# A selective-scan and feed-forward kernel on one Trainium2 core: scans from zero, first columns by ScalarE, shifted products, new places

## The chip, the cores and the metric

The kernel runs on one core of one Trainium2 chip. A core has five engines that run side by side: TensorE (PE in the profile; its weight loads are PEld), VectorE (DVE), ScalarE (ACT), GpSimd (POOL) and SyncE (SP, which here issues the DMAs). Each works through its own list of instructions in order, and an instruction waits on semaphores for what it needs from other engines and from DMAs. The metric is the device time of the program in microseconds (us), the median of several runs.

## The reference, cut to what matters

The input is two sequences of 4096 tokens with 256 features. The kernel computes a normalised selective-scan layer (Mamba-like) with a residual, and then a normalised feed-forward layer with ternary weights and a residual.

```python
xz = jnp.einsum('bld,ed->ble', x, W_in)            # x is layer-normed; 2 x 512 channels
x_path, z = jnp.split(xz, 2, axis=-1)
x_path = jax.nn.silu(x_path)
ssm = jnp.einsum('ble,se->bls', x_path, W_x)       # B, C (16 states each), dt, lam
...
dA = jnp.exp(A[None, None] * dt[..., None])
Bx = Br[:, :, None, :] * x_path[..., None]
u = (1.0 - lam_e) * dt_e * dA * Bx_prev + lam_e * dt_e * Bx
u = u.at[:, 0].set(dt_e[:, 0] * Bx[:, 0])
def step(h, inp):
    dA_, u_, C_ = inp
    h = dA_ * h + u_
    return (h, jnp.sum(h * C_[:, None, :], axis=-1))
_, ys = jax.lax.scan(step, h0, (dA_t, u_t, C_t))   # 512 channels x 16 states, 4096 steps
y = (y + x_path * D) * jax.nn.silu(z)
x = x + layernorm(einsum('ble,de->bld', y, W_out))
...
h = gelu(layer_norm(x) @ ternary(w1).T + b1)
x = x + layernorm(layer_norm(h) @ ternary(w2).T + b2)
```

## The kernel before

**Tiling.** The 8192 tokens are 16 blocks of T = 512 (`NB`), eight for each sequence; blocks 0 and 8 start a sequence (`s.first`). The scan of a block has 512 channels x 16 states = 8192 rows of 512 steps. A *unit* is one tile of 128 such rows: 32 channels (`G`) x 4 states. Block k has 64 units, numbered by j (four groups of 128 channels), q (four rounds of four states) and c (four sets of 32 channels within j). The four units of one (j, q) are a *group*; they share the tile `g` of 128 x 4 x 512, of which there are three (`GBUFS`).

**What a group does.** `decay` (ScalarE) makes da = exp(A dt) of one unit in PSUM, from the tile `dtr` (four decay tiles, `DA_PSUM`). `inputs` (GpSimd, L1046) makes the scan's input in `g`, the product of the tile `b` (the state's B, broadcast over the channels) and `vr` (the weighted x of the channels), in two halves of two units each. `unit_scan` (VectorE) runs the recurrence of a unit over the 512 steps with a starting value `ini`, a column of a small tile, or 0.0 in blocks 0 and 8. For the first `SPLIT[q]` units of a group (2, 1, 2, 1) the scan writes over da in PSUM (L1059), and VectorE multiplies it with C into `g` (`product_v`, L1076) and copies the last column into `hl` (L1077). For the other units the scan writes over `g` (L1062), ScalarE copies the last columns to `hl` (`last`, L1066), and GpSimd multiplies with C in place (`product_g`, L1072, 1024 or 1536 elements per partition). `sum_states` (TensorE, L1088) adds the states of a group by four matmuls into `y`, and `gate` (L1098) multiplies with silu(z). The tiles `b` and `c` are T + 2 columns wide and used from column 2.

**From block to block.** The state after the last step (`hl`) goes into the next block. Because u holds a term of the previous token, the start value is `hl` plus an outer product: `over`, `over_x`, `spread` and `carry` (L1023) make the outer product in the tile `ini`, and `initial` (GpSimd, L1032) adds `hl`, first for j = 0 and later for the rest.

**Order.** The instruction lists are written out by hand (`manual_schedule`); nothing is reordered afterwards. The main loop walks the units in order, and each unit has three *places*. While the scans of block k run, the front part of block k + 1 (`plan_ahead`: norm, projections, softplus, angles, B and C, the weighted x) and the back part of block k - 1 (`plan_behind`: output projection and the feed-forward layer) are issued piece by piece at the places of the table `AT` (192 places are one block); the front of block 0 takes its places from `AT_FIRST`, and the preparation of the ternary weights from `W_AT`. What belongs to a group comes at the lags of the table `LAG`, counted from the group's first unit. Decays and inputs are issued two units ahead of their scan (`AHEAD_DA`, `AHEAD_U`). The loads of `dtr` and `vr` for j + 1 (`load_ch`) stand in the main loop at the first unit of j, and the load of x of the block after the next at unit 60 (`X_AT`). All these DMAs go through SP's queue.

Of the kernel before, what the change touches and what calls it, by code (L numbers as in the profile page):

```python
# [8 lines left out]
F32 = mybir.dt.float32  # L9
# [5 lines left out]
P = 128  # L15
# [30 lines left out]
AHEAD_DA, AHEAD_U = 2, 2  # L46
X_AT = 60
# [4 lines left out]
    "product_v": (4,),  # L52
    "last": (24, 15, 21, 18, 13, 13, 18, 14, 19, 21, 21, 14, 15, 13, 19, 11),
    "product_g": (28, 17, 30, 19, 22, 17, 20, 26, 24, 21, 25, 20, 24, 13, 24, 15),
    "gate": (35, 38, 31, 26),
    "start": (18, 26, 27, 26),
    "sum": (32, 30, 36, 25, 36, 35, 24, 30, 31, 29, 28, 23, 45, 31, 29, 22),
}

W_AT = (1, 46, 70, 73, 74, 78, 85, 92, 103, 103, 106, 114, 116, 124, 141, 144, 149, 149, 153, 160, 160, 163, 163, 170, 174, 176, 180, 187, 188)  # L60
LOAD_FIRST = 6
AT = {
    "a_stats": (5, 5),
    "a_power": (5,),
    "a_offset": (8,),
    "a_apply": (8, 8),
    "a_turn": (15, 15),
    "a_evict": (16, 17),
    "project": (17, 24, 31, 31, 62, 66, 66, 76),
    "keep": (21, 25, 31, 35, 68, 72, 74, 78),  # L70
    "silu_x": (36,),
    "bc_project": (55, 60),
    "bc_take": (73,),
    "dt_project": (82,),
    "bc_square": (88,),
    "bc_power": (95,),
    "dt_row": (84,),
    "dt_spread": (92,),
    "softplus": (92,),
    "bc_scale": (137,),  # L80
    "dt_turn": (109, 115, 117, 117),
    "dt_keep": (117, 118, 118, 120),
    "dt_sum": (121,),
    "angles": (129,),
    "diag_lam": (118,),
    "silu_z": (153,),
    "sines": (153,),
    "rotate_a": (154,),
    "rotate_b": (154,),
    "bc_turn": (158,),  # L90
    "bc_store": (164,),
    "dot_sum": (176,),
    "dot_shift": (194,),
    "dot_take": (194,),
    "weigh": (141, 159, 194, 196),
    "weigh_x": (150, 167, 197, 197),
    "over": (121,),
    "over_x": (132,),
    "spread": (179,),
    "carry": (185,),  # L100
    "diag_dot": (196,),
    "skip": (198, 199, 199, 200),
    "skip_x": (198, 199, 200, 200),
    "load_dt": (124,),
    "load_v": (150,),
    "load_b": (167, 172, 172, 174),
    "load_c": (172, 184, 186, 189),
    "x_load": (4,),
    "out_project": (41, 49),
    "out_square": (47, 49),  # L110
    "out_power": (49, 54),
    "residual": (53, 54),
    "h_stats": (58, 58),
    "h_power": (63,),
    "h_offset": (65,),
    "h_apply": (68, 69),
    "h_turn": (78, 82),
    "h_evict": (78, 82),
    "ffn_1": (85, 93, 97, 98, 103, 107, 117, 129),
    "ffn_keep": (88, 94, 97, 106, 114, 115, 121, 135),  # L120
    "gelu": (133, 135),
    "ffn_2": (137, 150, 162, 190),
    "ffn_sums": (145, 159, 173, 191),
    "ffn_out": (146, 159, 175, 195),
    "ffn_square": (177, 160, 195, 196),
    "ffn_power": (180, 196),
    "ffn_scale": (189, 196),
    "finish": (189, 196),
# [3 lines left out]
    "a_stats": (-90, -90),  # L132
    "a_power": (-90,),
    "a_offset": (-90,),
    "a_apply": (-90, -90),
    "a_turn": (-90, -90),
    "a_evict": (-90, -90),
    "project": (-78, -77, -75, -72, 0, 12, 0, 3),
    "keep": (-76, -74, -71, -69, 0, 16, 0, 9),
    "silu_x": (-58,),  # L140
    "bc_project": (-70, -70),
    "bc_take": (-67,),
    "dt_project": (-66,),
    "bc_square": (-61,),
    "bc_power": (-60,),
    "dt_row": (-65,),
    "dt_spread": (-64,),
    "softplus": (-63,),
    "bc_scale": (-59,),
    "dt_sum": (-53,),  # L150
    "dt_turn": (-55, -55, -55, -55),
    "dt_keep": (-55, -55, -55, -55),
    "angles": (-52,),
    "diag_lam": (-54,),
    "silu_z": (56,),
    "sines": (-50,),
    "rotate_a": (-47,),
    "rotate_b": (-46,),
    "bc_turn": (-45,),
    "bc_store": (-44,),  # L160
    "dot_sum": (-30,),
    "dot_shift": (0,),
    "dot_take": (0,),
    "weigh": (-51, 0, 0, 2),
    "weigh_x": (-49, 0, 4, 8),
    "diag_dot": (0,),
    "skip": (1, 9, 0, 0),
    "skip_x": (2, 12, 0, 0),
    "load_dt": (-62,),
    "load_v": (-42,),  # L170
    "load_b": (-43, -20, 0, 7),
    "load_c": (-41, -20, 5, 20),
    "bc_project_first": (-73, -70, -69, -68),
    "decay_rates": (-57,),
# [4 lines left out]
def mamba_ffn_kernel(  # L179
# [287 lines left out]
    def weights_2(wide):  # L467
# [13 lines left out]
        def gains(h):  # L481
            if h == 0:
                nc.vector.tensor_add(b2bc, t["pb"], b2bc)
                t["row"] = small.tile([P, NH + 1], F32, tag="row", name="row", bufs=1)
            for f in range(4 * h, 4 * h + 4):
                nc.scalar.activation(
                    w[:, f, :],
                    q[:, f, :],
                    AF.Copy,
                    scale=t["g"][:, f : f + 1],  # L490
                    accum_out=t["row"][:, f : f + 1],
                )
# [61 lines left out]
    class Norm:  # L554


        def __init__(self, src, scale, eps, name):
            self.src, self.scale, self.eps, self.name = src, scale, eps, name
            self.mv = small.tile([P, NC4, 2], F32, tag="mv", name=f"mv_{name}")
            self.st = small.tile([P, NC4, 6], F32, tag="st", name=f"st_{name}")  # L560

        def stats(self, cs):
            for c in cs:
                nc.vector.bn_stats(self.st[:, c, :], self.src[:, c, :])
                nc.vector.bn_aggr(self.mv[:, c, :], self.st[:, c, :])
# [21 lines left out]
        def turn(self, kk):  # L587
            if kk == 0:
                self.oT = p1.tile([P, 2, T], F32, tag="oT", name=f"oT_{self.name}")
                self.pt = {}  # L590
# [11 lines left out]
    class Centred(Norm):  # L602


        def __init__(self, src, sums, scale, eps, name):
            self.src, self.sums, self.scale, self.eps, self.name = src, sums, scale / DM, eps, name
            self.nm = small.tile([P, NC4], F32, tag="nm", name=f"nm_{name}")
# [19 lines left out]
    class Block:  # L627
        pass

    def new_block(k):  # L630
# [5 lines left out]
        s.pz, s.dt, s.dtT, s.dx, s.vs, s.ph, s.bcq, s.ch, s.g = {}, {}, {}, {}, {}, {}, {}, {}, {}  # L636
        s.p2, s.ff, s.pq, s.ps, s.ys = {}, {}, {}, {}, {}
# [14 lines left out]
    def keep(s, e):  # L652
        if e == 0:
            s.xp = p1.tile([P, NJ, T], F32, tag="xp", name=f"xp_{s.k}")
            s.zs = {}
# [18 lines left out]
    def bc_project(s, cs):  # L674

        if cs[0] == 0:
            s.pbc = ps_ff.tile([P, NC4, 2 * NS + 2], F32, tag="ff", name=f"pbc_{s.k}")
# [73 lines left out]
    def softplus(s):  # L751
        if s.k == 0:
            special(freqs, freqs, AF.Softplus)

            nc.vector.tensor_scalar_mul(freqs, freqs, 1.0 / DI)
        for j in range(NJ):
            dt = p1.tile([P, T], F32, tag="dt", name=f"dt_{s.k}_{j}", bufs=4)
            special(dt, s.pb, AF.Softplus, scale=wdt[:, j : j + 1], bias=bdt[:, j : j + 1])
            nc.sync.dma_start(s.dt_d[j * P : (j + 1) * P, :], dt)
            s.dt[j] = dt  # L760
# [19 lines left out]
    def dt_turn(s, c):  # L780

        s.pq[c] = mm_tile([P, DI], f"pdtT_{s.k}_{c}")
        for j in range(NJ):
            nc.tensor.transpose(
                s.pq[c][:, j * P : (j + 1) * P], s.dt[j][:, c * P : (c + 1) * P], ident
            )

    def dt_keep(s, c):
        if c == 0:
            s.msum = small.tile([P, NC4], F32, tag="msum", name=f"msum_{s.k}")  # L790
# [7 lines left out]
    def angles(s):  # L798
# [3 lines left out]
        tn = small.tile([P, NC4, H], F32, tag="turns", name=f"tn_{k}", bufs=1)  # L802
        s.ang = small.tile([P, NC4, H], F32, tag="ang", name=f"ang_{k}")
        acc = pa[:, 3, 0, 0:NC4]
        s.cum = small.tile([P, NC4], F32, tag="cum", name=f"cum_{k}")
        nc.vector.tensor_copy(s.cum, acc)
        nc.vector.tensor_mul(
            ang,
            acc[:, :, None].to_broadcast([P, NC4, H]),
            freqs[:, None, :].to_broadcast([P, NC4, H]),  # L810
        )
        nc.vector.tensor_scalar(turns, ang, INV_2PI, ROUND, ALU.mult, ALU.add)
        nc.vector.tensor_scalar_sub(tn, turns, ROUND)
        for part in (PI2_HI, PI2_MID, PI2_LO):
            nc.vector.scalar_tensor_tensor(ang, tn, -part, ang, ALU.mult, ALU.add)
        nc.vector.tensor_scalar(s.ang, ang, -3.1415925, 3.1415925, ALU.max, ALU.min)
# [46 lines left out]
    def bc_store(s):  # L863
# [3 lines left out]
        s.blast = small.tile([NS, NQ], F32, tag="blast", name=f"blast_{s.k}")  # L867
        nc.scalar.activation(s.blast, round_of, AF.Copy, scale=bct[0:NS, T - 1 : T])
# [56 lines left out]
    def weigh(s, j):  # L925
# [5 lines left out]
            rhs=s.dt[j][:, 1:],  # L931
# [6 lines left out]
    def weigh_x(s, j):  # L938
        v = p1.tile([P, T], F32, tag="v", name=f"v_{s.k}_{j}", bufs=2)
        nc.vector.tensor_mul(v, s.ps.pop(j), s.xp[:, j, :])  # L940
        nc.sync.dma_start(s.v_d[j * P : (j + 1) * P, :], v)
# [14 lines left out]
    def over_x(s, prev):  # L956
        c4 = small.tile([P, NJ], F32, tag="c4", name=f"c4_{s.k}")
        nc.vector.tensor_mul(c4, s.po4, prev.xlast)
        s.c4 = c4

    def spread(s, prev):

        s.pov = mm_tile([P, NJ * NG + NQ], f"pov_{s.k}")
        for c in range(NG):
            nc.tensor.matmul(
                s.pov[:, 0 : NJ * NG].rearrange("p (j c) -> p j c", c=NG)[:, :, c],
# [5 lines left out]
        nc.tensor.matmul(s.pov[:, NJ * NG :], lhsT=state, rhs=prev.blast, start=True, stop=True)  # L972
# [636 lines left out]
```

## Time and profile before

| | us |
|---|---|
| median of 3 runs (lowest, highest) | 2003.9 (1998.66, 2006.47) |
| span of the profiled execution | 2000.2 |
| VectorE busy, share of the span | 1765.9, 88% |
| TensorE busy | 1779.9, 89% |
| GpSimd busy | 1750.2, 88% |
| ScalarE busy | 1625.3, 81% |
| mean granted TensorE clock | 0.953 of full speed |
| DMA, share of the 16 engines (hardware queue) | 47.8%, 230.80 MB |

The profile is of one execution. Busy times are the union of an engine's instructions; the ends of matmuls are modelled, and instructions that only wait or issue DMAs are not counted. In its rows, `out<-in` names tiles, then come partitions x elements and the count, the busy time and the mean duration in ns, and behind the second bar the engine's idle time just before these instructions with what ended most of it. The lines with L230 are ScalarE's activations, all recorded by one helper.

### The profile page before, as it was taken

The numbers are of one execution on the slowest core, as the hardware profiler recorded it, in microseconds if no ns is written. First come the engines' busy times: TensorE is split into PE (matmuls) and PEld (weight loads), VectorE is DVE, ScalarE is ACT, GpSimd is POOL, SyncE is SP. The second block draws the span as 40 slices with busy tenths as digits, with TensorE's granted clock in tenths as the row PEclk, the third lists the DMA queues.
The fourth block names the chain that finished last, engine by engine and source line by source line (L and its number), as shares of the span: only waits on it lengthen the run. The fifth ranks groups of instructions, "written<-read, shape, count | busy, mean of one in ns | idle before, by whom it ended". The sixth has DMA issues, their size and how long they took to land.

```text
span 2000.2 us, 28645 instructions
## 1 busy us (share of the span) xinstructions
PE 1779.9 (89%) x8910; PEld 1058.4 (53%) x8910; DVE 1765.9 (88%) x2714; ACT 1625.3 (81%) x3511; POOL 1750.2 (88%) x1063
## 2 busy tenths in 40 slices
PE   6866999999999999999999999999999999998788
PEld 3433555464645546464554646455464645545257
DVE  1778989999898999999899999989999998999961
ACT  4766897979789797978979797988979798896754
POOL 3689999999899999999999999999999999999970
PEclk7876999999999999999999999999999999999898
DMA  5733446365354636545463644546364454635400
GB/s 98 194 85 100 113 113 169 79 153 123 101 123 112 166 78 155 126 102 122 113 170 86 157 111 109 126 113 162 85 160 106 113 125 111 161 85 149 85 21 11
DMA packets 155721, 233.41 MB, mean 117 GB/s; under 512 B 30160, under 2 KB 55824, under 8 KB 155568
## 3 DMA queue, kind: packets, MB, share of 16 engines
q1 hardware_dynamic: 153440, 230.80, 47.8%
q0 software_dynamic: 544, 0.71, 0.3%
q8 instruction: 70, 1.15, 0.3%
q14 instruction: 83, 0.68, 0.1%
q10 hardware_dynamic: 1584, 0.07, 0.1%
HBM read 188.51 MB, written 42.99 MB: 116 GB/s over the span
## 4 chain that ended last, share of the span: by engine, by line
DVE 41%; ACT 27%; PE 12%; issue 12%; POOL 3%; DMA 3%; SPq 0%; DVEq 0%; ACTq 0%; POOLq 0%
DVE g L1062 16%; DVE da L1059 12%; ACT da L230 7%; ACT L228 5%; DVE g L1076 4%; PE pf L1162 3%; ACT L230 2%; PE pz L644 2%; ACT dt L230 2%; POOL g L1046 2%; ACT zs L230 2%; DVE dx L989 1%; PE pf L1171 1%; DVE zs L1098 1%; ACT h L230 1%
## 5 line engine op out<-in xcount | busy, mean ns | idle before, releaser
L1046 POOL TENSOR_TENSOR g<-b,vr 128x1024 f32<-128x1024 f32 x512 | 1016.2, 2000 | 44.9 <-PE y L1088 22.5
L230 ACT ACTIVATE da<-dtr,aneg 128x512 f32<-128x512 f32 x1024 | 680.2, 681 | 33.6 <-DVE hl L1077 18.2
L1062 DVE TENSOR_TENSOR_SCAN g<-da,ini,g 128x512 f32<-128x512 f32 x560 | 688.4, 1267 | 19.8 <-ACT da L230 19.1
L1072 POOL TENSOR_TENSOR g<-c,g 128x1024 f32<-128x1024 f32 (+1 forms) x256 | 626.5, 2452 | 88.6 <-ACT hl L1066 69.1
L1059 DVE TENSOR_TENSOR_SCAN da<-da,ini,g 128x512 f32<-128x512 f32 x336 | 429.3, 1278 | 39.6 <-ACT da L230 32.9
L1088 PE MATMUL y<-g,fold 128*32 128x512 f32 x2048 | 339.7, 630 | 39.8 <-POOL g L1072 28.0
L1162 PE MATMUL pf<-w2q,h 128*128 128x257 f32 x1024 | 313.1, 387 | 15.5 <-DVE o L1200 11.8
L1076 DVE TENSOR_TENSOR g<-da,c 128x512 f32<-128x512 f32 x384 | 264.1, 688 | 17.6 <-DVE da L1059 0.5
L644 PE MATMUL pz<-oT_a,wi 128*128 128x512 f32 x512 | 243.3, 617 | 33.0 <-ACT zs L662 28.6
L1139 PE MATMUL ph<-oT_h,w1q 128*128 128x512 f32 x480 | 250.7, 654 | 22.0 <-ACT h L1150 17.1
L1171 PEld LDWEIGHTS pf<-h 128*128 128x128 f32 x1024 | 194.8, 190 | 26.9
L1171 PE MATMUL pf<-h 128*128 128x128 f32 x1024 | 196.9, 274 | 0.0
L1162 PEld LDWEIGHTS pf<-w2q,h 128*128 128x128 f32 x1024 | 155.2, 192 | 59.0 <-DVE o L1200 43.1
L644 PEld LDWEIGHTS pz<-oT_a,wi 128*128 128x128 f32 x512 | 91.5, 193 | 173.8 <-issue 74.3
L1139 PEld LDWEIGHTS ph<-oT_h,w1q 128*128 128x128 f32 x480 | 88.6, 202 | 178.5 <-issue 79.3
L1088 PEld LDWEIGHTS y<-g,fold 128*32 128x32 f32 x2048 | 53.3, 110 | 176.7 <-POOL g L1072 82.9
L1066 ACT COPY hl<-g 128x2 f32<-128x2 f32 (+1 forms) x256 | 47.0, 184 | 104.4 <-DVE g L1062 100.1
L228 ACT ACT_TABLE_LOAD x98 | 125.7, 1283 | 1.7
L1108 PE MATMUL po<-wo,zs 128*128 128x256 f32 x480 | 112.8, 389 | 0.0
L1108 PEld LDWEIGHTS po<-wo,zs 128*128 128x128 f32 x480 | 89.7, 192 | 37.1 <-ACT xp L662 11.8
L928 PE MATMUL ps<-dt,ident 128*128 128x511 f32 x128 | 73.0, 654 | 28.8 <-DVE remdot L890 25.1
L1062 DVE TENSOR_TENSOR_SCAN g<-da,g 128x512 f32<-128x512 f32 x80 | 93.7, 1207 | 2.7 <-ACT da L230 2.6
(232 smaller groups left out, 2460.2 us busy)
## 6 DMA issues: line engine op xcount, KB each, us to landing
dtr<-dt_d SPq DMA_DIRECT2D x256, 256.0 KB, 4.8
vr<-v_d SPq DMA_DIRECT2D x256, 256.0 KB, 7.3
dt_d<-dt SPq DMA_DIRECT2D x64, 256.0 KB, 2.1
v_d<-v SPq DMA_DIRECT2D x64, 256.0 KB, 2.8
b<-bc_d SPq DMA_DIRECT2D x256, 64.0 KB, 2.1
c<-bc_d SPq DMA_DIRECT2D x256, 64.0 KB, 2.2
xpre<-in_L_attn_x_dram SPq DMA_DIRECT2D x16, 512.0 KB, 4.4
xpost<-in_L_attn_x_dram SPq DMA_DIRECT2D x15, 512.0 KB, 4.6
```

The lines of the kernel that those rows point to most:

```text
L228: nc.scalar.preload_act_table_set(name)
L230: nc.scalar.activation(dst, src, f, **kw)
L644: nc.tensor.matmul(s.pz[e], lhsT=wi[:, kk, e * P : (e + 1) * P], rhs=s.na.oT[:, kk, :], start=(kk == 0), stop=(kk == 1),)
L1046: nc.gpsimd.tensor_mul(s.g[j, q][:, hs, :], s.bcq[0, q][:, None, :].to_broadcast([P, 2, T]), s.ch[j, "vr"][:, hs, :],)
L1059: nc.vector.tensor_tensor_scan(da, da, g, ini, ALU.mult, ALU.add)
L1062: nc.vector.tensor_tensor_scan(g, da, g, ini, ALU.mult, ALU.add)
L1072: nc.gpsimd.tensor_mul(g, s.bcq[1, q][:, None, :].to_broadcast([P, NG - n, T]), g)
L1076: nc.vector.tensor_mul(s.g[j, q][:, c, :], da, s.bcq[1, q])
L1088: nc.tensor.matmul(s.ys[j][c * G : (c + 1) * G, :], lhsT=fold, rhs=g[:, c, :], start=False, stop=(q == NQ - 1), skip_group_check=True,)
L1139: nc.tensor.matmul(s.ph[f], lhsT=w1q[:, kk, f * P : (f + 1) * P], rhs=s.nh.oT[:, kk, :], start=(kk == 0), stop=(kk == 1),)
L1162: nc.tensor.matmul(po[:, 0 : DM + 1], lhsT=gT, rhs=w2q[:, f, :], start=(f == 0), stop=(f == NH - 1), skip_group_check=True,)
L1171: nc.tensor.matmul(po[:, DM + 1 :], lhsT=gT, rhs=gT, start=False, stop=False, skip_group_check=True,)
```

## The change

It has five parts.

- *Scans from 0.* `unit_scan` always starts from 0.0. In blocks other than 0 and 8 the first column of a group's inputs is set to the state after the first step instead: dA(0) x (start value) + u(0). `carry` makes dA(0) (`da0`) and u(0) (`u0`) as small tiles of 128 x 64, from the first columns of dt and of the weighted x, which `weigh_x` and `over_x` copy into a wider `c4` and `spread` spreads with it; `initial` multiplies and adds. `enter` (ScalarE) copies the four columns of a group into `g`.
- *Inputs.* `inputs` makes all four units by one instruction, from column 1 on (511 columns) where `enter` fills the first column.
- *Columns.* `g` gets rows of T + 2 columns; inputs and scans stand at columns 2 to 513, and the products with C are written to columns 0 to 511. The tile `c` is used from column 0, `b` from column 2 as before.
- *Places.* Decays, inputs, `enter` and `product_v` get a lag for each unit or group in `LAG` (`AHEAD_DA`, `AHEAD_U` go). The loads of `dtr` and `vr` of all j, `initial`, and the load of x become pieces of the plan with places in `AT`; `angles` becomes seven pieces. All numbers of `LAG`, `W_AT`, `AT` and `AT_FIRST` are new.
- *Bookkeeping.* Tiles are made by whichever piece comes first (`own`), `dt` is one tile for the four j, and `g` is released after both `last` and `sum_states` (`leave`).

```diff
-AHEAD_DA, AHEAD_U = 2, 2
-X_AT = 60
 LAG = {
-    "product_v": (4,),
-    "last": (24, 15, 21, 18, 13, 13, 18, 14, 19, 21, 21, 14, 15, 13, 19, 11),
-    "product_g": (28, 17, 30, 19, 22, 17, 20, 26, 24, 21, 25, 20, 24, 13, 24, 15),
...
-    "sum": (32, 30, 36, 25, 36, 35, 24, 30, 31, 29, 28, 23, 45, 31, 29, 22),
+    "decay": (-8, -3, -4, -11, 0, -6, -5, -3, -2, -5, -3, 1, -3, -16, -4, -3,
...
+    "inputs": (-7, -4, -6, 0, -2, -1, 0, -2, -12, -2, -13, -6, -7, -9, -5, -1,),
+    "enter": (-8, -4, -8, -6, -3, -3, -8, -6, -10, -12, -14, 0, 1, -13, -12, -3,),
+    "product_v": (5, 7, 4, 4, 16, 4, 4, 4, 6, 3, 4, 4, 5, 4, 4, 4, 7, 9, 4, 4,
...
+    "last": (24, 18, 18, 19, 26, 18, 23, 18, 13, 18, 21, 8, 19, 16, 28, 21,),
+    "product_g": (26, 21, 12, 21, 13, 15, 17, 19, 12, 17, 16, 15, 19, 14, 22, 18,),
...
+    "sum": (34, 24, 19, 22, 22, 27, 22, 22, 20, 26, 21, 22, 45, 21, 30, 21,),
 }
 AT = {
...
-    "load_dt": (124,),
-    "load_v": (150,),
-    "load_b": (167, 172, 172, 174),
-    "load_c": (172, 184, 186, 189),
+    "load_dt": (153, 231, 272, 315,),
+    "load_v": (157, 184, 261, 324,),
+    "load_b": (171, 180, 197, 224,),
+    "load_c": (162, 185, 196, 225,),
...
     def bc_store(s):
...
-        s.blast = small.tile([NS, NQ], F32, tag="blast", name=f"blast_{s.k}")
-        nc.scalar.activation(s.blast, round_of, AF.Copy, scale=bct[0:NS, T - 1 : T])
+        s.blast = small.tile([NS, 2, NQ], F32, tag="blast", name=f"blast_{s.k}")
+        for i in range(1 if s.first else 0, 2):
+            t = i * (T - 1)
+            nc.scalar.activation(s.blast[:, i, :], round_of, AF.Copy, scale=bct[0:NS, t : t + 1])
...
     def weigh_x(s, j):
...
+        if not s.first:
+            s.own("c4", lambda: small.tile([P, 3, NJ], F32, tag="c4", name=f"c4_{s.k}"))
+            nc.scalar.copy(s.c4[:, 2, j : j + 1], v[:, 0:1])
...
     def load_bc(s, q, ms):
...
+            t = t[:, 2:] if m == 0 else t[:, 0:T]
...
     def carry(s):
...
+        s.da0 = scan.tile(whole, F32, tag="da0", name=f"da0_{s.k}")
+        s.u0 = scan.tile(whole, F32, tag="u0", name=f"u0_{s.k}")
+        nc.vector.tensor_mul(s.da0, dt0.to_broadcast(whole), aneg)
+        nc.vector.tensor_mul(s.ini, over.to_broadcast(whole), ends[:, 0, None, :, None].to_broadcast(whole))
+        nc.vector.tensor_mul(s.u0, v0.to_broadcast(whole), ends[:, 1, None, :, None].to_broadcast(whole))
+        special(s.da0, s.da0, AF.Exp)
 
     def initial(s, prev, j):
 
         js = slice(j, j + 1) if j == 0 else slice(j, NJ)
         nc.gpsimd.tensor_add(s.ini[:, js], s.ini[:, js], prev.hl[:, js])
+        nc.gpsimd.tensor_mul(s.ini[:, js], s.ini[:, js], s.da0[:, js])
+        nc.gpsimd.tensor_add(s.ini[:, js], s.ini[:, js], s.u0[:, js])
 
-    def inputs(s, j, q, h):
-
-        if h == 0:
-            s.g[j, q] = scan.tile([P, NG, T], F32, tag="g", name=f"g_{s.k}_{j}_{q}", bufs=GBUFS)
-        hs = slice(2 * h, 2 * h + 2)
+    def states(s, j, q):
+        if (j, q) not in s.g:
+            s.g[j, q] = scan.tile([P, NG, T + 2], F32, tag="g", name=f"g_{s.k}_{j}_{q}", bufs=GBUFS)
+        return s.g[j, q]
+
+    def inputs(s, j, q):
+
+        t0 = 0 if s.first else 1
         nc.gpsimd.tensor_mul(
-            s.g[j, q][:, hs, :],
-            s.bcq[0, q][:, None, :].to_broadcast([P, 2, T]),
-            s.ch[j, "vr"][:, hs, :],
+            states(s, j, q)[:, :, 2 + t0 :],
+            s.bcq[0, q][:, None, t0:].to_broadcast([P, NG, T - t0]),
+            s.ch[j, "vr"][:, :, t0:],
         )
 
+    def enter(s, j, q):
+
+        nc.scalar.copy(states(s, j, q)[:, :, 2], s.ini[:, j, q, :])
+
     def unit_scan(s, j, q, c):
 
-        da, g = das[s.k, j, q, c], s.g[j, q][:, c, :]
-        ini = 0.0 if s.first else s.ini[:, j, q, c : c + 1]
+        da, g = das[s.k, j, q, c], s.g[j, q][:, c, 2:]
...
-            nc.vector.tensor_tensor_scan(da, da, g, ini, ALU.mult, ALU.add)
+            nc.vector.tensor_tensor_scan(da, da, g, 0.0, ALU.mult, ALU.add)
...
-            nc.vector.tensor_tensor_scan(g, da, g, ini, ALU.mult, ALU.add)
+            nc.vector.tensor_tensor_scan(g, da, g, 0.0, ALU.mult, ALU.add)
...
     def product_g(s, j, q):
...
-        nc.gpsimd.tensor_mul(g, s.bcq[1, q][:, None, :].to_broadcast([P, NG - n, T]), g)
+        nc.gpsimd.tensor_mul(
+            g[:, :, 0:T], s.bcq[1, q][:, None, :].to_broadcast([P, NG - n, T]), g[:, :, 2:]
+        )
...
     def product_v(s, j, q, c):
...
-        nc.vector.tensor_mul(s.g[j, q][:, c, :], da, s.bcq[1, q])
+        nc.vector.tensor_mul(s.g[j, q][:, c, 0:T], da, s.bcq[1, q])
```

## The prediction

> **What bounds the kernel now.** I read the page's busy shares first, then the VectorE timeline to find where each block of 512 tokens begins (its first scan), then the stage table cut at those starts, and last the rows of scans and GpSimd products. The starts are 59.84, 196.11, 312.55, ... 896.13, 1012.58, 1126.39, ... 1825.87, and the last scan group ends near 1937.1. So the 2000.2 us of span are 59.8 of prologue, 136.3 for block 0, 1629.8 for blocks 1 to 14, 111.3 for block 15 and 63.1 of tail. A normal block takes 116.5 us. The stage table, for block 7 (normal) and block 8 (first of the second sequence, so its 64 scans already start from 0):
>
> ```profile
> core 0: us, PE busy (x) PEld busy (x) DVE busy (x) ACT busy (x) POOL busy (x), PEclk, DMA share, GB/s
> 896.13:1012.58 116.45, 105.35 (x526) 60.74 (x526) 109.57 (x170) 100.08 (x216) 107.80 (x64) 0.99 0.52 122
> 1012.58:1126.39 113.81, 107.45 (x554) 63.82 (x554) 105.76 (x171) 99.84 (x217) 107.24 (x64) 0.99 0.52 125
> ```
>
> No engine has much room: VectorE is busy 109.6 of 116.45 us, GpSimd 107.8, TensorE about 107 (its ends are modelled), ScalarE 100.1. VectorE is the fullest, and block 8 shows that it sets the pace: with 3.8 us less VectorE work and the other engines as before, the block is 2.6 us shorter. The waits of VectorE in a block add up to 5 to 6 us, most of them for a decay (the chain of waits has VectorE's scans as its largest item, 16% and 12%).
>
> ```profile
> L1062 DVE TENSOR_TENSOR_SCAN g<-da,ini,g 128x512 f32<-128x512 f32 x560 | 688.4, 1267 | 19.8 <-ACT da L230 19.1
> L1059 DVE TENSOR_TENSOR_SCAN da<-da,ini,g 128x512 f32<-128x512 f32 x336 | 429.3, 1278 | 39.6 <-ACT da L230 32.9
> L1062 DVE TENSOR_TENSOR_SCAN g<-da,g 128x512 f32<-128x512 f32 x80 | 93.7, 1207 | 2.7 <-ACT da L230 2.6
> L1046 POOL TENSOR_TENSOR g<-b,vr 128x1024 f32<-128x1024 f32 x512 | 1016.2, 2000 | 44.9 <-PE y L1088 22.5
> L1066 ACT COPY hl<-g 128x2 f32<-128x2 f32 (+1 forms) x256 | 47.0, 184 | 104.4 <-DVE g L1062 100.1
> ```
>
> A scan that reads its initial value from a column takes 60 ns more than one that starts from the constant 0 (1267 against 1207; the other kind 1278 against 1220). Durations of neighbours overlap, so I also looked at rows of three in a stretch; the second column is what the three take together:
>
> ```profile
> 1008.85 3.62 DVE L1062 TENSOR_TENSOR_SCAN g<-da,ini,g 128x512 f32<-128x512 f32 x3
> ...
> 1027.14 3.44 DVE L1062 TENSOR_TENSOR_SCAN g<-da,g 128x512 f32<-128x512 f32 x3
> ```
>
> 0.18 us for three: the 60 ns are there in the pitch too.
>
> **The change, part by part, for one normal block.**
>
> *Scans from 0 (VectorE).* 64 scans x 0.060 = -3.8 us. Added: two products of 128x64 in `carry`; the one already there (L1023) took 0.20, so +0.4. `angles` is cut in seven pieces with the same instructions. VectorE: 109.6 - 3.8 + 0.4 = 106.2.
>
> *Inputs as one instruction (GpSimd).* Two of 1024 become one of 4x511. The price of a form comes from two rows, the third is a product in which both operands and the result stand at the same column of their tiles:
>
> ```profile
> L1072 POOL TENSOR_TENSOR g<-c,g 128x1536 f32<-128x1536 f32 x128 | 371.9, 2905 | 65.8 <-ACT hl L1066 63.6 <-ACT dtc L721 1.9 <-DMA vr<-v_d 0.3
> L1072 POOL TENSOR_TENSOR g<-c,g 128x1024 f32<-128x1024 f32 x128 | 255.7, 1998 | 22.8 <-DMA vr<-v_d 10.2 <-issue 6.1 <-ACT hl L1066 5.5
> ...
> L425 POOL TENSOR_TENSOR wide<-wide 128x1024 f32<-128x1024 f32 x4 | 9.4, 2349 | 0.0
> ...
> L748 POOL TENSOR_TENSOR bc<-bc,ms 128x128 f32<-128x128 f32 x16 | 6.4, 402 | 0.6 <-ACT xlast L668 0.6
> ```
>
> 512 more elements cost 907 ns, 1.77 ns each, and 184 ns are fixed. One input of 2044 is 184 + 2044 x 1.77 = 3.80 us, against 1016.2/256 = 3.97 for the pair: 16 x -0.17 = -2.7. Bounds: L425 has 2.11 ns per element (4.50 us), L748 1.70 (3.66). I take 1.77, because the reads of b and v keep the distance of two columns that they have at L1046 (3 and 1, before 2 and 0); only the result moves, to b's column. `initial` gets four more instructions, 2 x (0.22 + 0.285) = +1.0 by its own rows. GpSimd: 107.8 - 2.7 + 1.0 = 106.1.
>
> The Trainium skill speaks against this: "GPSIMD Engine Reference", section 3.1, gives 4497 ns for a product of two inputs of 2048 elements, and calls some 2.5 cycles per element the floor for two inputs. The rows of L1046 and L1072 are below that floor, L425 is at it. By the page's figure the inputs would be 16 x 4.5 = 72 us instead of 61, and GpSimd would be over 117.
>
> *Product with C two columns ahead (GpSimd, VectorE).* Same counts and elements. C stands at column 0, the read of g at 2 plus two for each row of 514, the result two before it. Bounds as above: 1.70 and 2.11 ns per element, -1.3 and +7.0 us per block over 8 products of 1024 and 8 of 1536. I take none, since the reads stay at different columns as in the row of L1072. VectorE's product (0.69) only writes elsewhere: none.
>
> *First columns by ScalarE.* 16 copies of 128x4, five of `c4`, one more of `blast`, at 0.184 (L1066), and an Exp of 128x64 at some 0.2 (the sines of 128x32 take 0.218): 22 x 0.184 + 0.2 = +4.2. ScalarE: 100.1 + 4.2 = 104.3. These lie in ScalarE's idle 16 us; without that cover they cost 4.2 us a block. `enter` waits for the sums that last read the buffer and for `ini`; behind it stand the decays, for which VectorE waits at once, with four decay buffers as reserve.
>
> *Buffers and order.* With three g buffers, a group's scans now wait for 3.80 us of inputs instead of 1.97 for the first half. The tightest place is the last group of a block, which takes the buffer of two groups before: product 2.9, three sums 1.8, inputs 3.8 = 8.5 us in a row, against some 7 us of VectorE's work on the group between; before, 6.7. That is 1 to 1.5 us of wait per block unless other VectorE pieces lie there. The new places answer by sums some ten places earlier. The loads of dt, v and x become planned pieces: the same DMAs on SP's queue (16 + 16 + 32 + 1 a block), later in it, and 4.8 to 7.3 us to landing. The second dt tile stands only three places ahead of its first decay in the written order, but behind nothing that waits later than the block's first groups, some 20 us before it is used. Zero; each us beyond that cover is a us of ScalarE. TensorE gets one small matmul less and wider ones: zero.
>
> *Sum.* VectorE and GpSimd both come to 106.2. What a placement reaches is read from the two stages above: the fullest engine is busy 109.57/116.45 = 94.1% and 107.24/113.81 = 94.2%. 106.2/0.942 = 112.7 per block. Thirteen normal blocks: 13 x -3.8 = -49; block 8: -1.1; block 15: 64 x 0.06 = -3.8; the start +1.8, as the first scan waits for whole inputs. Together -52: the span goes from 2000.2 to 1948. The profiled span lies 3.7 under the median 2003.9 (no other time of that execution is given), so the time is about 1951. Its own range: if VectorE keeps the waits of blocks 7 and 8 (6.9 and 8.05 us), 113.1 to 114.3, up to 1975; at 1.70 ns and 5 us of wait, 111.2, down to 1930.
>
> **The rivals.**
>
> *ScalarE becomes the bound (slower).* Place: its queue, where 23 more instructions stand among 64 decays and the copies that wait for scans. It idles 16.4 us in a block. If that idle time stays, because it is in-order waits, a block takes 104.3 + 16.4 = 120.7: 14 x 4.2 = +59, some 2060. It decides for a loss from 12.2 us of idle time on (116.5 - 104.3). For it: in block 8 ScalarE still idled 14.0. Against: 6 to 8 us of it are copies that wait for scans because ScalarE is early. Chance 0.14.
>
> *GpSimd gets slower (slower).* If inputs cost 4.50, GpSimd is at 106.1 + 11.2 = 117.3, and with 3 us of waits a block takes 120: 14 x 3.8 plus as much in blocks 0 and 15, some 2065; with the products at 2.11 too, 2160. For it: L425, and no row here writes at an odd column with rows of 514. Against: the distance of the reads. Chance 0.11.
>
> *The gain is spent in waits.* The whole inputs and new order cost VectorE 2 to 4 us more of waiting per block, 115 to 117: 1980 to 2010. Chance 0.16.
>
> *GpSimd gets faster.* At 1.70 or less, and fewer waits: under 1930. Chance 0.06.
>
> *The scans don't get cheaper.* Block 8 excludes it.
>
> **How the numbers follow.** Forecast 0.53, rivals 0.14, 0.11, 0.16, 0.06. About 0.5%, 10 us, is what can be told from no change here: faster (under 1994) is 0.53 + 0.06 + half of 0.16 = 0.67, within 0.08, slower 0.25. The range leaves out a tenth above and a tenth below: 1928 to 2062. The likeliest case's own range is 1930 to 1975.
>
> **What would show it.** Scan rows near 1207 and 1220 without `ini`; inputs near 3.8 us (wrong at 4.5) and products at 2.0 and 2.9; ScalarE some 104 us per block; blocks at 112 to 114; VectorE's waits for inputs no more than 2 us a block. The prediction is wrong if VectorE's idle time grows past 9 us a block, or GpSimd's busy time past 108.

## The result, and the profile after

The changed kernel takes 2009.2 us (median of 20 runs, 1996.9 to 2019.8), the kernel before 2003.4 (20 runs, 1998.6 to 2006.5). The ratio is 1.0032, with a 95% interval of 1.0019 to 1.0045: 0.3% slower, where 2.6% faster was forecast. The profiled execution has a span of 2004.9 us, against 2000.2, at a mean granted TensorE clock of 0.932, against 0.953. Cut at the first scan of each block as before (block 15 is counted up to the start of its last scan, at 1937.1 and 1941.5; that scan ends 1.2 us later):

| us | before | forecast | after |
|---|---|---|---|
| prologue and block 0 | 59.8 + 136.3 | +1.8 | 55.9 + 125.8 |
| blocks 1 to 14 | 1629.8 | -50.4 | 1647.0 |
| block 15 and tail | 111.3 + 63.1 | -3.8 | 112.8 + 63.4 |
| span | 2000.2 | 1948 | 2004.9 |

The start is 14.4 us shorter, and the fourteen blocks in the middle are 17.3 us longer instead of 50 shorter. The stage table of two of them (us, then busy time and instruction count of each engine):

```profile
core 0: us, PE busy (x) PEld busy (x) DVE busy (x) ACT busy (x) POOL busy (x), PEclk, DMA share, GB/s
770.77:887.11 116.34, 107.59 (x556) 65.88 (x556) 105.32 (x173) 102.86 (x240) 110.68 (x53) 0.97 0.51 123
887.11:1006.19 119.08, 106.40 (x526) 63.40 (x526) 105.00 (x170) 101.95 (x231) 110.95 (x50) 0.94 0.49 121
```

VectorE has become lighter by 4.3 us (109.6 to 105.3, 106.2 forecast), and ScalarE heavier by less than feared (100.1 to 102.9). But GpSimd went from 107.8 to 110.7 where 106.1 was forecast. It is now the fullest engine, at 95% of the shorter kind of block. The longer kind takes 118.6 to 119.6 us. In the one shown GpSimd waits 3.6 us before the block's third input (2.6 in the shorter), VectorE waits 1.9 us for the sums in `y` (0.2), and the granted TensorE clock is 0.94 (0.97). Which rows of GpSimd grew:

```profile
L1076 POOL TENSOR_TENSOR g<-b,vr 128x2044 f32<-128x2044 f32 x224 | 852.9, 3812 | 84.1 <-DMA b<-bc_d 31.6 <-ACT rsf L232 27.5 <-PE pt_a L596 12.0
...
L1111 POOL TENSOR_TENSOR g<-c,g 128x1536 f32<-128x1536 f32 x128 | 419.4, 3277 | 8.7 <-DVE g L1095 7.2 <-PE po L1151 1.2 <-POOL g L1111 0.3
...
L1111 POOL TENSOR_TENSOR g<-c,g 128x1024 f32<-128x1024 f32 x128 | 279.3, 2182 | 0.6 <-DVE g L1095 0.6
```

Inputs cost 3.81 us, as worked out (3.80). The products with C cost 2182 and 3277 ns, before 1998 and 2905: +184 and +372 ns, as if one row of 512 in the small form and two in the large had become slower by 185 each. Eight of each per block make +4.4 us. VectorE's scans are as forecast, and their waits have changed hands, from decays to inputs (behind the second bar: idle time, then who ended most of it):

```profile
L1095 DVE TENSOR_TENSOR_SCAN g<-da,g 128x512 f32<-128x512 f32 x640 | 758.2, 1208 | 14.1 <-ACT da L232 14.0
...
L1092 DVE TENSOR_TENSOR_SCAN da<-da,g 128x512 f32<-128x512 f32 x384 | 464.9, 1223 | 107.3 <-POOL g L1076 80.2
```

### The profile page after: what moved, and what is told of

Same layout as the page of the kernel before. It is cut to its first block, busy times and chain, and to the rows that moved or that the text cites. A ratio compares the mean times of both kernels' runs of the same rounds, so it can differ in the third digit from the quotient of the medians.

```text
span 2004.9 us, 28574 instructions
## 1 busy us (share of the span) xinstructions
PE 1792.3 (89%) x8938; PEld 1090.3 (54%) x8938; DVE 1704.2 (85%) x2742; ACT 1665.6 (83%) x3833; POOL 1794.4 (90%) x863
## 5 line engine op out<-in xcount | busy, mean ns | idle before, releaser
L1076 POOL TENSOR_TENSOR g<-b,vr 128x2044 f32<-128x2044 f32 (+1 forms) x256 | 975.7, 3817 | 101.1 <-DMA b<-bc_d 31.6
L1095 DVE TENSOR_TENSOR_SCAN g<-da,g 128x512 f32<-128x512 f32 x640 | 758.2, 1208 | 14.1 <-ACT da L232 14.0
L1111 POOL TENSOR_TENSOR g<-c,g 128x1024 f32<-128x1024 f32 (+1 forms) x256 | 695.9, 2729 | 9.3 <-DVE g L1095 7.7
L1092 DVE TENSOR_TENSOR_SCAN da<-da,g 128x512 f32<-128x512 f32 x384 | 464.9, 1223 | 107.3 <-POOL g L1076 80.2
L651 PE MATMUL pz<-oT_a,wi 128*128 128x512 f32 x512 | 259.8, 649 | 13.5 <-DVE xpost L1175 13.3
L1182 PE MATMUL ph<-oT_h,w1q 128*128 128x512 f32 x480 | 226.3, 611 | 3.9 <-ACT dtT L796 3.8
L651 PEld LDWEIGHTS pz<-oT_a,wi 128*128 128x128 f32 x512 | 100.1, 207 | 143.4 <-issue 86.2
L1129 PEld LDWEIGHTS y<-g,fold 128*32 128x32 f32 x2048 | 50.3, 110 | 149.8 <-POOL g L1111 63.1
L927 PE MATMUL pw<-ddot,dtT 128*128 128x128 f32 (+1 forms) x512 | 79.8, 301 | 58.0 <-DVE dx L1007 39.0
L927 PEld LDWEIGHTS pw<-ddot,dtT 128*128 128x128 f32 x512 | 67.9, 200 | 90.8 <-DVE dx L1007 56.5
L927 PEld LDWEIGHTS ps<-mix,dtT 128*128 128x128 f32 x512 | 80.8, 224 | 37.7 <-issue 37.0
```

The source lines that it names most:

```text
L651: nc.tensor.matmul(s.pz[e], lhsT=wi[:, kk, e * P : (e + 1) * P], rhs=s.na.oT[:, kk, :], start=(kk == 0), stop=(kk == 1),)
L927: nc.tensor.matmul(ps[:, c * P - 1 + skip : c * P - 1 + n], lhsT=s.dtT[c][:, j * P : (j + 1) * P], rhs=diag[:, c, skip:], start=start and ...
L1076: nc.gpsimd.tensor_mul(states(s, j, q)[:, :, 2 + t0 :], s.bcq[0, q][:, None, t0:].to_broadcast([P, NG, T - t0]), s.ch[j, "vr"][:, :, t0:],)
L1092: nc.vector.tensor_tensor_scan(da, da, g, 0.0, ALU.mult, ALU.add)
L1095: nc.vector.tensor_tensor_scan(g, da, g, 0.0, ALU.mult, ALU.add)
L1111: nc.gpsimd.tensor_mul(g[:, :, 0:T], s.bcq[1, q][:, None, :].to_broadcast([P, NG - n, T]), g[:, :, 2:])
```

## The experiments

A row of `g` has 514 columns, 2056 bytes, 8 more than a multiple of 16. C stands at column 0 and g is read from column 2, so row r of `g` is read 8 + 8r bytes away from C, up to multiples of 16: row 1 by 16, row 2 by 24, row 3 by 32. (Where the tiles start is not in the record; that they start at multiples of 16 bytes is taken here, and the counts of slow rows below fit it.) The product of 1024 covers rows 2 and 3, that of 1536 rows 1 to 3. If a distance of a multiple of 16 bytes is what costs, one and two rows are slow, which is the count in the trace. The first four runs test this, and what the scans alone are worth.

**Rows of 516 columns.**

```diff
-            s.g[j, q] = scan.tile([P, NG, T + 2], F32, tag="g", ...
+            s.g[j, q] = scan.tile([P, NG, T + 4], F32, tag="g", ...
```

Inputs, scans and products keep their columns, with the ends written out (`2 : T + 2`).

> The changed kernel with rows of g of 516 columns in place of 514, so that every row stands 8 bytes past a multiple of 16 as C's column 0 reads it; nothing else is changed. Theory A (GpSimd's product with C is slow for each row whose read of g lies a multiple of 16 bytes from C, and GpSimd sets the pace): products back to 2.00 and 2.91 us, GpSimd some 106 us busy per block, blocks of 112 to 114.5, time 1945 to 1975. Theory B (whole inputs and the new order cost the gain in waits): products faster, but blocks stay at 115.5 or more and VectorE's wait for inputs stays near 4 to 5 us a block, time 1990 to 2010.

1978.6 us, ratio to the kernel before 0.9877 (0.9861 to 0.9894). The rows of its products and one of its blocks:

```profile
L1111 POOL TENSOR_TENSOR g<-c,g 128x1536 f32<-128x1536 f32 x128 | 373.3, 2916 | 12.8 <-DVE g L1095 9.1 <-ACT da L232 1.8 <-POOL g L1111 0.5
...
L1111 POOL TENSOR_TENSOR g<-c,g 128x1024 f32<-128x1024 f32 x128 | 256.3, 2002 | 2.7 <-DVE g L1095 2.2
```

```profile
core 0: us, PE busy (x) PEld busy (x) DVE busy (x) ACT busy (x) POOL busy (x), PEclk, DMA share, GB/s
644.11:759.99 115.88, 106.38 (x556) 66.45 (x556) 105.32 (x173) 102.72 (x240) 106.59 (x53) 0.96 0.50 124
```

The products are back, GpSimd is at 106.6, and 30.6 us of time are won by eight bytes per row. It beats both kernels. But the blocks stay near 115.9, not 112 to 114.5: neither theory is right alone. GpSimd's rate explains the larger half of the miss (30.6 of the 58 us between 2009.2 and the forecast 1951), and the rest lies in waits.

**C at column 2 again.**

```diff
-            t = t[:, 2:] if m == 0 else t[:, 0:T]
+            t = t[:, 2:]
```

> The changed kernel with C read from column 2 of its tile again; rows of g stay 514. If a distance of a multiple of 16 bytes between the two reads makes a row slow, one row of each group's product is slow (row 2): products of 1024 stay at 2.18, those of 1536 come to 3.09; GpSimd 109.2 us per block, time some 1990 to 2000. If only a multiple of 32 bytes did, no row would be slow: 2.00 and 2.91, time as in the run with rows of 516.

1993.4 us, 0.9953 (0.9938 to 0.9968).

```profile
L1111 POOL TENSOR_TENSOR g<-c,g 128x1536 f32<-128x1536 f32 x128 | 396.8, 3100 | 5.7 <-DVE g L1095 4.7 <-PE po L1151 1.0
L1111 POOL TENSOR_TENSOR g<-c,g 128x1024 f32<-128x1024 f32 x128 | 279.7, 2185 | 3.1 <-DVE g L1095 3.1
```

2185 and 3100 against 2002 and 2916: one slow row in each. With C at 8 bytes, the rows lie 8, 16 and 24 bytes apart, and only row 2 is on a multiple of 16. A rule of 32 bytes would have left none slow, if the tiles start at multiples of 32. It fails in the changed kernel wherever they start: rows 1 and 3 of the large product are 16 bytes apart in their distance, and both are slow.

**The kernel before, scans from 0.** `ini = 0.0` in all blocks.

> The kernel before with all scans from 0.0: leaves out the state that is carried from one block to the next, all other work stays. If VectorE sets the pace before the change, the 13 blocks that carried a state come to 113.8 us as block 8 did and block 15 loses 2 to 4 us: time 1963 to 1968. If another engine holds the block, 1990 to 2000.

1965.5 us, 0.9813 (0.9798 to 0.9828), and all blocks from 1 to 14 take 113.6 to 114.2. So the scans alone are worth 38 us in the old order, and block 8 was the right sample.

**The kernel before, C at column 0.**

```diff
-                    t[n * G : (n + 1) * G, 2:],
+                    t[n * G : (n + 1) * G, (2 - 2 * m) : (2 - 2 * m) + T],
...
-            s.bcq[m, q] = t[:, 2:]
+            s.bcq[m, q] = t[:, (2 - 2 * m) : (2 - 2 * m) + T]
```

> The kernel before with C read from column 0 of its tile, in line with g: only GpSimd's (and VectorE's) product with C can change. Theory A: products 2.35 and 3.43 us (2.11 ns per element), GpSimd 114.8 us per block and 118 to 122 us blocks, time 2030 to 2090. If the column of C does not matter: 2004, and the slow product of the changed kernel has another cause.

2041.9 us, 1.0182 (1.0157 to 1.0208); blocks of 117.4 and 120. Here every row lies in line with C, and every row is slow:

```profile
L1072 POOL TENSOR_TENSOR g<-c,g 128x1536 f32<-128x1536 f32 x128 | 443.6, 3466 | 25.7 <-ACT hl L1066 14.6 <-ACT dtc L721 10.9
...
L1072 POOL TENSOR_TENSOR g<-c,g 128x1024 f32<-128x1024 f32 x128 | 302.5, 2363 | 18.9 <-DMA vr<-v_d 13.3 <-issue 3.2 <-DMA dtr<-dt_d 1.0
```

That is 183 ns per row again ((2363 - 1998)/2; (3466 - 2905)/3 = 187). The row of L425 in the kernel before, a subtraction whose two reads are also in line, has nearly the same price (2349 ns for 1024 elements).

The next runs look for the rest: with rows of 516 no engine is over 92% of a block (106.6 of 115.9), where 94% was taken.

**One load earlier.** In the run with rows of 516, GpSimd waits 3.1 us once a block for the third input. SP's timeline shows its `b` behind eight loads of `c` that took 6.8 us.

```diff
-    "load_b": (171, 180, 197, 224,),
+    "load_b": (171, 180, 181, 224,),
```

> Rows of 516 columns, and one place moved: the load of b for the third round (q = 2) of a block goes from place 197, behind the load of c for the same round, to 181, ahead of it. In the run with rows of 516 GpSimd waits some 3.1 us once a block for the third input of the block; on SP's queue that load of b stood behind eight loads of c that took 6.8 us because they wait for GpSimd's products of the block before. If the load is what is waited for and GpSimd's queue sets the pace, the wait goes and blocks lose 1.5 to 3 us: 1940 to 1958. If the slack is taken up elsewhere, 1973 to 1979.

1979.1 us, 0.9878 (0.9861 to 0.9894): nothing. GpSimd's waits before and after the move (engine, line, waited for: total us, times, longest):

```profile
POOL g L1076 <- ACT rsf L232: 39.6, 14, 3.1
POOL g L1076 <- DMA b<-bc_d: 36.6, 8, 8.6
POOL g L1076 <- PE y L1129: 26.7, 34, 3.5
POOL g L1076 <- PE pt_a L596: 23.7, 7, 4.1
```

```profile
POOL g L1076 <- ACT rsf L232: 39.5, 14, 3.1
POOL g L1076 <- PE y L1129: 26.7, 30, 3.5
POOL g L1076 <- ACT xp L668: 17.0, 10, 2.0
POOL g L1111 <- DVE g L1095: 16.7, 16, 2.8
```

The load's waits are gone from blocks 1 to 14 (those put down to `pt_a` were the same wait, named by what came last), and others grew. GpSimd with 9 us of idle time per block does not set the pace alone.

**Sums earlier.** The 2.9 us under `rsf` are the input of group (3, 1), which waits for the sums of group (2, 2); on TensorE these stood behind `ffn_2`.

```diff
-    "sum": (34, 24, 19, 22, 22, 27, 22, 22, 20, 26, 21, 22, 45, 21, 30, 21,),
+    "sum": (34, 24, 19, 22, 22, 27, 22, 22, 20, 26, 16, 22, 45, 21, 30, 21,),
```

> Rows of 516 columns, and one place moved: the sums of group (2, 2) go from lag 21 to 16, ahead of the first output matmuls of the feed-forward layer (ffn_2, 5.6 us on TensorE) instead of behind them. GpSimd waits 2.9 us once a block for the buffer that these sums release. If that order is what is waited for and GpSimd sets the pace, blocks lose 1 to 2.5 us: 1945 to 1965. If the feed-forward matmuls that now come 2 us later cost VectorE as much, 1973 to 1982.

2034.5 us, 1.0156 (1.0141 to 1.0172): 56 us worse than with rows of 516 alone, beyond either expectation. That wait is gone, but VectorE now waits 81.1 us in all for the results of `ffn_2` (51.9) and 72.7 for inputs (45.4). One group's sums, moved by five places, cost some 4 us a block (blocks of 115.6 to 122.6). The order has no slack at that place.

**Inputs in halves.** Two instructions of 2x511, one behind the other.

> Rows of 516 columns, and inputs again as two instructions of two units each, one right behind the other, so that the scans of the first two units may start 1.9 us earlier; GpSimd is busy 2.7 us a block more. If whole inputs are what keeps VectorE waiting (45 us in all in the run with rows of 516), that wait halves and the time is 1955 to 1970. If GpSimd's queue sets the pace, the extra 2.7 us a block cost 10 to 35 us: 1985 to 2015.

1986.6 us, 0.9929 (0.9904 to 0.9955). VectorE's waits for inputs fell from 45.4 to 7.7 us in all, and the time rose by 8, so whole inputs are not what holds VectorE. GpSimd was busy 2.0 us a block more, and the block that begins at 648 still takes 115.4 us, with GpSimd at 108.6, 94% of it. So GpSimd's queue does not set the length of such a block either; the added time lies in blocks 0, 1, 8, 9 and 15.

**Without the copies of first columns.** No `enter`, no copies into `c4`; this leaves the carried state out.

> Rows of 516 columns, and the 21 ScalarE copies per block that put first columns in place are left out (16 of enter, 5 into c4; c4's parts are zeros from a small GpSimd memset); inputs are 512 wide. Leaves out the state carried from block to block. If these copies hold the block at 115.9 us (by their time on ScalarE, 3.9 us a block, or by what they wait for), blocks come to 112 to 113.8 and the time to 1935 to 1955. If the new order as a whole does, with its waits spread over all engines, blocks stay at 115 or more: 1968 to 1980.

1976.8 us, 0.9876 (0.9859 to 0.9892): 1.8 us less than with them, and by the ratios nothing. Over the whole run these copies are free in the changed kernel's order, and the rival that ScalarE becomes the bound has fallen. Single blocks differ more: they take 113.7 to 118.5 us.

**Scans from 0 in the old order.** Three versions of the kernel before with the first columns taken over: `spread`, `carry` and `initial` from the changed kernel, the inputs in halves from column 1, and a ScalarE copy for each group.

```diff
+        if h == 0 and not s.first:
+            nc.scalar.copy(s.g[j, q][:, :, 0], s.ini[:, j, q, :])
...
-    "weigh": (141, 159, 194, 196),
-    "weigh_x": (150, 167, 197, 197),
+    "weigh": (141, 159, 168, 172),
+    "weigh_x": (150, 167, 172, 176),
```

> The kernel before with its own places, columns and halves, and only the scans from 0 with what they need taken over: first columns by a ScalarE copy per group, the wider c4, spread, carry, and initial as in the changed kernel (its first part at place 186); the last two pieces of the weighted x move from places 194 to 197 up to 168 to 176, as their first columns are needed by then. If scans from 0 gain what block 8 showed and ScalarE has room for 4 us more, blocks take 113.5 to 115 and the time is 1962 to 1982. If ScalarE's queue becomes the bound, 116 or more a block, 2000 or more.

2172.9 us, 1.0848 (1.0832 to 1.0865). ScalarE stands still for what its new copies need, with the decays behind them:

```profile
ACT c L945 <- DVE v L943: 121.6, 56, 6.9
ACT g L1070 <- PE y L1108: 64.0, 40, 3.9
...
ACT da L231 <- DVE da L1040: 55.3, 14, 7.2
```

The second version takes these out of ScalarE's way: VectorE copies into `c4`, the Exp of `da0` comes later, and `enter` one unit later.

> As the run that took scans from 0 over into the old order, but ScalarE's new work no longer stands in front of decays where it has to wait: the first columns of the weighted x are copied by VectorE (4 x 0.15 us a block), the Exp of da0 comes behind carry as a piece at place 187, and a group's first columns are copied one unit ahead of its first scan, not two. In the run before, ScalarE waited 121.6 us for the weighted x, 64 us for buffers and 55 us for carry. If these waits were the loss, blocks take 113.5 to 116 and the time is 1965 to 1995. If ScalarE simply has no room for the copies, 118 or more a block: over 2030.

2125.7 us, 1.0620 (1.0604 to 1.0636). The first wait is gone, but GpSimd waits 135.4 us for sums and TensorE 52.1 us in `spread`. So the move of `weigh` was tried alone, on the kernel before (the diff above without the copy):

> The kernel before with one thing moved: the last two pieces of the weighted x (weigh, weigh_x for j = 2, 3) from places 194 to 197 up to 168 to 176, where scans from 0 need them. If the move alone crowds TensorE's and VectorE's queues at the end of a block, blocks go from 116.5 to 120 or more (2050 or more), and that is what the taken-over versions lost; if it costs little, 2004 to 2015, and ScalarE's copies are the loss.

2015.9 us, 1.0066 (1.0051 to 1.0081): some 12 us, not the 120 that were missing. Last, the pieces were put back and only their first columns spread late (four more matmuls of 128x2 at place 203, one product at 207):

> As the mended version in the old order, but the last two pieces of the weighted x stay at their old places 194 to 197; their first columns are spread by a second set of four small matmuls at place 203 and multiplied at 207, since the start values of j = 1 to 3 are finished only at place 228. Computes the reference. If the move of these pieces was the loss, blocks of 114 to 117 and 1970 to 2010. If the copies into g, which wait for buffers in ScalarE's queue, are the loss, 120 or more: over 2060.

2042.6 us, 1.0198 (1.0181 to 1.0215), blocks of 119.3 with no engine busy over 109.1. This version leaves nothing out and is 77 us slower than the old order with the carried state left out. Neither expectation holds as written: the block lies between. Putting the pieces back, with their first columns spread late, won 83 us, where the move alone cost 12 in the kernel before. VectorE still waits 37.8 us in all for the copies, and GpSimd 26.7 for `carry`. How much of the 39 us above the kernel before each of them costs is not shown.

## Why the prediction was wrong

*Scans from 0* was right: 1208 and 1223 ns, VectorE 105.3 us a block (106.2 forecast), and 38 us where nothing else changed.

*Inputs as one instruction* was right: 3.81 us. The rule of the Trainium skill that was weighed there ("GPSIMD Engine Reference", section 3.1, 4497 ns for 2048 elements) does not hold for these operands: 3847 ns for 2048 here. (The figure there is of an addition, and the floor in that section is some 2.6 cycles.) For rows in line it comes close: worked out from the 2363 and 3466 ns above, 2048 elements would take an estimated 4.57 us; no run has that size in line. The row of L425, from which the prediction took its upper bound, is a subtraction, not a product.

*First columns by ScalarE* was right in size (102.9 us against 104.3) and in costing nothing in the changed kernel's order (1.8 us). The first taken-over version shows what the rival meant: in an order not made for them the same copies wait, and hold up the decays behind them.

*Product with C two columns ahead* is the step that failed: "I take none, since the reads stay at different columns as in the row of L1072". Different columns are not enough. The reads must not lie a multiple of 16 bytes apart, and with rows of 514 that holds for some rows only. The text had the two addresses ("two plus two for each row of 514") and a bound of +7.0 us, but took the rate as one for all rows. The term was +4.4 us a block instead of 0, and 30.6 us of time by the run with rows of 516. The rival "GpSimd gets slower" named the right engine, but its condition, inputs of 4.50 us, did not come; the products became slower. 110.7/0.942 = 117.5 by the prediction's own rule, measured 116.0 to 119.6. Both signs that the prediction gave for being wrong came: GpSimd is past 108 us a block (110.7), and VectorE's idle time is past 9 (116.34 - 105.32 = 11.0).

*What a placement reaches* failed too. "94.2%" was read from stages of the old order and given to a new one. With the product mended, the fullest engine is at 92.0% (106.6 of 115.9), 3.2 us a block above the forecast 112.7. Blocks 1 to 14 take 1622.7 us there, 43 above the forecast. The start gave back some 16 of it (-14.4 where +1.8 was forecast, an order of the prologue that I did not price), which is luck. For this half of the miss the rival "The gain is spent in waits" was right: it had 2 to 4 us more of VectorE's waiting and blocks of 115 to 117, and with the product mended VectorE idles 10.6 us in a block of 115.9, before 6.9 of 116.45.

What in the new order makes these waits is not settled. The late load of `b`, whole inputs and ScalarE's copies were each taken away and moved the time by -2 to +8 us. VectorE's 10.6 idle us in a block are spread over eleven kinds of waits, none above 2.0. Other orders were not searched.

One rival that no run tested stands in the traces: the granted TensorE clock. In the run with rows of 516 all of blocks 1 to 14 but one hold a stretch of 3.4 us at half clock, 75 to 81 us after their first scan. The exception is block 8. Here are that stretch in the block that begins at 644 (the last number but two, 0.50, is the granted clock), two groups of its matmuls, and then the same two groups in block 8:

```profile
721.14:724.55 3.41, 3.41 (x17) 1.83 (x15) 3.05 (x7) 3.40 (x4) 3.33 (x4) 0.50 0.00 0
721.38 1.93 PE L927 MATMUL ps<-mix,dtT 128*128 128x128 f32 x8
723.24 1.69 PE L1129 MATMUL y<-g,fold 128*32 128x512 f32 x8
...
1068.81 1.05 PE L927 MATMUL ps<-mix,dtT 128*128 128x128 f32 x8
1069.79 1.06 PE L1129 MATMUL y<-g,fold 128*32 128x512 f32 x8
```

At half clock the two groups take 3.5 us together instead of 2.0, and `ffn_2` stands right behind them. VectorE then waits 1.5 us for its result, a wait that block 8 does not have; block 8 takes 113.7 us. Block 8 also has no copies of first columns, but without these copies the blocks still differ: the four without such a stretch take 113.7 to 114.5 us, the ten with one 114.0 to 118.5. In the old order with scans from 0, blocks 2 to 12 take 113.8 us with and without one. So the new order seems to feel a loss on TensorE that the old one absorbs. No run changed the clock alone, so this is not shown as a cause. At the 1.4 us by which the block at 644 falls behind block 8 at this wait, thirteen blocks would be an estimated 18 of the 43 us.

*Buffers and order* named the tight place at the end of a block and 1 to 1.5 us of wait for inputs a block; VectorE waits 80.2 us in all for inputs, more than 5 a block (1.7 in the block shown with rows of 516). The range (1928 to 2062) held the time; the forecast of a gain did not.

## What to carry to other kernels

When a product reads two streams, compute the distance of the two start addresses for each row of the access pattern, not only for the first: a pad that shifts rows against each other can bring single rows back into line. When several engines are above 90% of a stage, work taken off one of them is worth only what the next fullest and the order allow; price the added work of every engine by its own rows, and do not carry a utilisation from one order to another. Work put on an engine with idle time is free only behind nothing late: here the same copies cost at most 2 us in one order and had a part in a loss of more than 100 in another.

## What the runs showed of the hardware

- GpSimd's product of two f32 streams costs some 185 ns more for each row of 512 elements whose two reads lie a multiple of 16 bytes apart: 0, 16 and 32 are slow, 8 and 24 are not (1998 to 2002 ns for two rows with none slow, 2182 to 2185 with one, 2363 with both). The Trainium skill gives 16 bytes as the cacheline of SBUF ("Advanced Engine Details and Errata", SBUF Cachelines), which fits the period; no run shows that it is the cause.
- The column of the result made no difference to GpSimd: inputs were written at 12, 20, 28 and 36 bytes past a multiple of 2048 in the four rows and took 3.81 us, and a start at an odd column cost nothing that shows. In the run with rows of 516 each row of the product is written in line with C, and none is slow (2002 ns): it is the two reads that count.
- VectorE's product with C fell from 688 to 673 ns in the changed kernel. It did not in the kernel before with C at column 0 (687), and it did with C at column 2 in the changed one (672), so C's column is not the reason; what is stays open.
- The granted TensorE clock fell to 0.50 in single stretches of a block. In one of 3.4 us a group of eight matmuls of 128x128 took 1.93 us, against 1.05 in a block without such a stretch there (run with rows of 516).
